# Attention with experts on one core: the pairs that scatter lose ScalarE's transfers and GpSimd's multiply, and one transfer spreads both heads' sums

## The chip, the core and the metric

The kernel runs on one core of a Trainium2 chip. The core has TensorE (PE, with PEld for the loading of weights), VectorE (DVE), ScalarE (ACT), GpSimd (POOL), SyncE (SP), which here only issues transfers, and 16 DMA engines. The metric is the device time of one launch in microseconds (us), as the median of several runs.

## The reference

A transformer block over x of shape [8, 512, 256] (8 batches, 512 tokens, 256 channels), all in float32. Cut to what matters:

```python
xn = layernorm(x)
kv = (xn @ w_kv_down) @ w_kv_up            # latent of 128, then k and v
q = xn @ w_q                               # 16 heads of 64
att = softmax(causal(q @ k.T / 8))         # per head, 512 x 512
attn = (att @ v) @ w_out
...
# experts: 8 of hidden size 128, every token takes its best 2
y = (silu(t @ gate[e].T) * (t @ up[e].T)) @ down[e].T
ffn = sum over the two experts of y * mean weight of the expert, + shared expert
return x + attn + ffn
```

## The kernel before, in words

The work on attention is cut into 64 *pairs*: 8 batches times 8 pairs of heads. The loop of line 906 goes over them, m = 0 to 63. A pair's work, with the names and lines that the profile shows:

- `keys` (L578) and `queries` (L587) multiply k and q on TensorE into PSUM, and ScalarE copies them out (L580, L592). `values` (L568) does this for v.
- `scores` (L615) multiplies q and k on TensorE, one 128-row query chunk and one head at a time. VectorE adds the causal mask and takes the row's extreme in one instruction (L622), and ScalarE takes the exponential and the row sums (L629).
- `transposed` (L642, L649) turns the 128x128 blocks in 32x32 squares on VectorE, into the tile `blk`. The squares are right inside, but lie on the wrong partitions. `moved` (L654) puts that right with 16 transfers `pt<-blk` of 80 KB, each from 32 partitions to 32 others. It gives each to a queue: SP's, GpSimd's or ScalarE's.
- `inverse_sums` (L674) takes the inverse of the row sums (L678), transposes them (`riT`, L681) and has GpSimd's queue store them as the tile `row` in DRAM (L683), 16 KB with pieces of 128 bytes.
- `spread_sums` (L686) reads `row` back, repeated over 64 partitions, into `rb`. It is two transfers on SP's queue (L691), one for each head, 128 KB each in pieces of 512 bytes.
- `weighted` (L696) multiplies the probabilities `pt` with v on TensorE (PV, `ps_y`, L704), two pairs later than their scores. ScalarE copies the result from PSUM into `yT` (L716), and GpSimd multiplies that by `rb` (L717). In the very last pair VectorE does both in one multiply from PSUM (L714).
- `project` (L729) multiplies `yT` of a whole batch with `w_out`.

The tiles `blk`, `pt` and `rb` have two buffers each, `rs` three and `row` four.

Other work is put between by a plan. `put(m, place, f)` says that f runs in pair m at a place from 0 to 2 within it. The layer norms, the router (L313) and the making of weights fill pairs 0 to 13. Then come the *scatter pairs*, m = 14 to 21. In each, four of the 32 token tiles are sent to their two experts' lists in DRAM by `scatter_rows` (L446): two indirect transfers by GpSimd (L449), each followed by a small memset (L457). From pair 22 on (E0, L885) the experts' 39 tiles are fetched, multiplied (L500, L512, L525) and added into the output in DRAM (L536), spread evenly over 67 half-pairs that begin at half-pair 49.

In a scatter pair the 16 transfers `pt<-blk` are shared so: 1 by GpSimd, 5 by ScalarE, which issues them in the next pair right after `weighted` has been called there, and 10 by SP. In other pairs it is 5 by GpSimd and 11 by SP, in the last two pairs 8 and 8. GpSimd's order of instructions is that of the program; the order within every engine follows that of the calls. In the compiled program the transfers of SP's queue take eight semaphores in turn, so that each waits for the one eight places before it to have landed; ScalarE's and GpSimd's queues do the same with theirs.

Of the kernel before, what the change touches and what calls it, by code (L numbers as in the profile page):

```python
# [32 lines left out]
F32 = mybir.dt.float32  # L33
# [7 lines left out]
P = 128  # L41
# [7 lines left out]
def kernel(  # L49
# [17 lines left out]
    nc = tc.nc  # L67

    B, T, C = x.shape
# [3 lines left out]
    D = 64  # L73
# [6 lines left out]
    NTILE = NT // P  # L80
    NQ = T // P
    VH = 4
    QB = 32
    NB = P // QB
# [9 lines left out]
    rowp = ctx.enter_context(tc.tile_pool(name="rowp", bufs=4, space=DRAM))  # L94
# [8 lines left out]
    rbp = ctx.enter_context(tc.tile_pool(name="rbp", bufs=2))  # L103
# [6 lines left out]
    def bank(shape, name):  # L110
        return ps_w.tile(shape, F32, tag="w", name=name)
# [139 lines left out]
    lats, qs, ks, vs, pts, rss, rbs, blks = {}, {}, {}, {}, {}, {}, {}, {}  # L251
    yTs, rows, shared = {}, {}, {}
# [382 lines left out]
    def transposed(b, p, i, pr):  # L635

        if (b, p) not in blks:
            blks[b, p] = blkp.tile([P, NB, 2, NBLK, QB], F32, name="blk")
        blk = blks[b, p]
        nr = min(i + 1, NQ - 1)  # L640
        for j in range(2):
            nc.vector.transpose(  # L642
                blk[:, :, j, i : i + (nr - 1) * (NQ - 1) + 1 : NQ - 1, :].rearrange(
                    "p b c q -> p c b q"
                ),
                pr[:, j, : nr * P].rearrange("p (c b k) -> p c b k", b=NB, k=QB),
            )
            if i == NQ - 1:
                nc.vector.transpose(  # L649
                    blk[:, :, j, 7, :],  # L650
                    pr[:, j, nr * P :].rearrange("p (b k) -> p b k", k=QB),
                )

    def moved(b, p, by_pool, by_act=0):  # L654


        pt = ptp.tile([P, NB, 2, NBLK, QB], F32, name="pt")

        def begin(by, k):
            a, kb = divmod(k, NB)  # L660
            by.dma_start(pt[ts(kb, QB), a], blks[b, p][ts(a, QB), kb])  # L661

        left = []
        for k in range(NB * NB):
            if k * by_pool % 16 < by_pool:
                begin(nc.gpsimd, k)
            elif k % 3 == 1 and len(left) < by_act:
                left.append(k)
            else:
                begin(nc.sync, k)  # L670
        pts[b, p] = pt
        return lambda: [begin(nc.scalar, k) for k in left]

    def inverse_sums(b, p):  # L674


        ri, riT = ris[p % len(ris)]
        nc.vector.reciprocal(  # L678
            ri[:, : 2 * NQ], rss[b, p].rearrange("p j i -> p (j i)")
        )  # L680
        nc.vector.transpose(riT, ri)  # L681
        row = rowp.tile([NB, QB, QB], F32, name="row")
        nc.gpsimd.dma_start(row.rearrange("a x q -> (a x) q"), riT)  # L683
        rows[b, p] = row

    def spread_sums(b, p):  # L686

        rb = rbp.tile([P, NB, NQ * QB], F32, name="rb")
        for j in range(2):
            row = rows[b, p][:, ts(j, NQ), :].rearrange("a i q -> a (i q)")  # L690
            nc.sync.dma_start(  # L691
                rb[ts(j, D)], row.unsqueeze(0).broadcast_to([D, NB, NQ * QB])
            )
        rbs[b, p] = rb

    def weighted(b, p, final=False):  # L696


        ps = bank([P, NB, NQ, QB], "ps_y")
        for c in range(NQ):  # L700
            for j in range(2):
                h = 2 * p + j
                at = at_ci[c, c]
                nc.tensor.matmul(  # L704
                    ps[ts(j, D), :, c:, :],
                    vs[b, h // VH][:, c, ts(h % VH, D)],
                    pts[b, p][:, :, j, at : at + NQ - c, :],
                    start=(c == 0), stop=(c == NQ - 1),
                )
        yT = ytp.tile([P, T], F32, name="yT")  # L710
        y = yT.rearrange("p (i a q) -> p a i q", a=NB, q=QB)
        rb = rbs[b, p].rearrange("p a (i q) -> p a i q", q=QB)
        if final:
            nc.vector.tensor_tensor(y, ps, rb, ALU.mult)  # L714
        else:
            nc.scalar.copy(y, ps)  # L716
            nc.gpsimd.tensor_tensor(y, y, rb, ALU.mult)  # L717
        yTs[b, p] = yT
# [48 lines left out]
    def put(m, place, f, *a):  # L767
        if place >= 2:
            m, place = m + 1, place - 2
        plan.setdefault(m, []).append((place, len(plan[m]) if m in plan else 0, f, a))  # L770

    pairs = [(b, p) for b in range(B) for p in range(NPAIR)]
    LAG = 2
    products = {}
    for m, (b, p) in enumerate(pairs):
        if m + 1 < len(pairs):
            put(m, 0.22, keys, *pairs[m + 1])
            put(m, 0.24, queries, *pairs[m + 1])
        if m < BLOCK0:
            put(m + 1, 0.32, inverse_sums, b, p)  # L780
        put(m + 1, 1.32 if m + 1 < BLOCK0 else 0.34, spread_sums, b, p)
        if m + LAG < BLOCK0:
            put(m + LAG, 1.4, weighted, b, p)
        else:
            products[m + LAG] = (b, p)
        put(m, 1.25 if m < BLOCK0 else 0.26, values, b, p * 2 // VH, p % 2)
    for b in range(B):
        m = b * NPAIR
# [82 lines left out]
    for k in range(12):  # L871
        put(R0 + k // 4, 0.35 + 0.5 * (k % 4), lambda: next(steps, None))
    S0 = R0 + 3
    for n in range(NTILE):
        put(S0 + n // NQ, 0.35 + 0.5 * (n % NQ), scatter_rows, n)


    def begin_experts():
# [3 lines left out]
        ep = tmp_pools.enter_context(tc.tile_pool(name="ep", bufs=1))  # L882
        xouts = ep.tile([P, NQ, C], F32, name="xout")

    E0 = S0 + NTILE // NQ  # L885
    END = len(pairs) - 5
    put(E0, 0.1, begin_experts)
    first, n_halves = 2 * E0 + 5, 2 * (END - E0) - 7
    for t in range(NET):
# [8 lines left out]
        put_half(2 * END + b, 0.7, bring_out, b)  # L898
    put_half(2 * END + B - 1, 0.7, bring_back)

    scattering = range(S0, S0 + NTILE // NQ)
    ordered = ExitStack()
    last = []
    rest = []
    assert BLOCK0 <= S0
    for m in range(len(pairs) + 1):
        if m == 0:
            ordered.enter_context(tc.manual_schedule(engines={nc.gpsimd.engine}))
        todo = sorted(plan.pop(m, ()), key=lambda e: e[:2])
        for g, group in enumerate(((0, 3), (1, 2)) if m < BLOCK0 else ()):  # L910
            chunks, exps = scores(*pairs[m], group)
            for chunk in last:
                transposed(*chunk)
            last = chunks
            if g == 0 and m > 0:
                moved(*pairs[m - 1], 5)
            for e in exps[:2]:
                e()
            del exps[:2]
            for place, _, f, a in todo:  # L920
                if (place >= 1) == g:
                    if place - g > EARLY:
                        while exps:
                            exps.pop(0)()
                    f(*a)
                    if exps:
                        exps.pop(0)()
            while exps:
                exps.pop(0)()
        if m < BLOCK0:  # L930
            continue

        chunks, exps = [], []
        if m < len(pairs):
            chunks, exps = scores(*pairs[m], (3, 1))
            for chunk in last:
                transposed(*chunk)
            if last:
                moved(*pairs[m - 1], 5)
            last = []  # L940
            exps.pop(0)()
            exps.pop(0)()
            transposed(*chunks.pop(0))
            weighted(*products.pop(m))
            more = scores(*pairs[m], (2, 0))
            exps.pop(0)()
            exps.pop(0)()
            transposed(*chunks.pop(0))
            chunks, exps = more
        for f in rest:  # L950
            f()
        rest = []


        for place, _, f, a in todo + [(2, 0, lambda: None, ())]:
            if place > EARLY - 0.07:
                while exps:
                    exps.pop(0)()
            if place > HALF and chunks:
                while chunks:  # L960
                    transposed(*chunks.pop(0))
                inverse_sums(*pairs[m])
                if m in scattering:
                    rest = [moved(*pairs[m], 1, 5)]
                else:
                    moved(*pairs[m], 8 if m >= len(pairs) - 2 else 5)
            f(*a)
            if exps:
                exps.pop(0)()


    weighted(*products.pop(len(pairs)))
    for tt in range(NQ):
        project(B - 1, tt, pss[tt], first=NS + NPAIR - 3, last=NS + NPAIR - 1)
    assert not plan and products.keys() == {len(pairs) + 1}, (plan, products)
    weighted(*pairs[-1], final=True)
    for tt in range(NQ):
        project(B - 1, tt, pss[tt], first=NS + NPAIR - 1)
    ordered.close()
# [45 lines left out]
```

## Time and profile before

| what | value |
|---|---|
| median of three runs | 987.74 us (986.42 to 988.87) |
| the profiled execution's own time | 987.82 us |
| its span, first to last instruction | 986.1 us |
| mean granted TensorE clock | 0.978 of full speed |
| busy: TensorE / VectorE / ScalarE / GpSimd | 933.2 / 596.4 / 506.9 / 597.5 us |
| moved by the DMA engines | 190.63 MB in 127594 packets |

The span is shorter than the time of the execution by the 1.7 us around the first and the last instruction. Busy time counts instructions that compute or that issue indirect and GpSimd transfers; issues by SP and ScalarE are in the chain of waits and the lists of transfers instead. In a row "A L1 <- B L2" the first is who waited, the second what ended the wait. "Queue" names such as q0 (GpSimd's), q1 (SP's) and q10 (ScalarE's) come with the share of the 16 DMA engines' span that their packets took. "SPq", "ACTq" and "POOLq" in the chain are the issuing of transfers by those engines.

### The profile page before, as it was taken

The page shows a single profiled execution, that of the slowest core. Times are in us where ns is not written, and L with a number is a line of the kernel's source. Part 1 is how long each engine was busy: PE and PEld are TensorE (multiplying, and loading weights), DVE is VectorE, ACT ScalarE, POOL GpSimd, SP SyncE. Part 2 cuts the span into 40 slices and gives each one's busy share as a digit, 9 for nine tenths or more (in the row PEclk, how much of TensorE's full clock was granted, in tenths as well). Part 3 has the DMA queues.
Part 4 walks back from the last instruction along what each step waited for, and adds up shares of the span by engine and source line. Part 5 has one row for each costly group of instructions (what it writes and reads, how often), then busy time and mean ns, then how long its engine had stood idle before and what let it go on. Part 6 is the DMA issues. An engine that isn't in the chain of part 4 may idle for free.

```text
span 986.1 us, 16151 instructions
## 1 busy us (share of the span) xinstructions
PE 933.2 (95%) x4326; PEld 562.6 (57%) x4326; DVE 596.4 (60%) x2160; ACT 506.9 (51%) x1468; POOL 597.5 (61%) x819
## 2 busy tenths in 40 slices
PE   8898999997679889999999999999999999999997
PEld 3454555643346435675666756576556775557555
DVE  3986783796543567446664456754567546674660
ACT  2564464544443456445664556644467544664550
POOL 2587676346677764646676566675757747665450
PEclk9899899999789999999999999999999999999999
DMA  7489788675566768867787677886778868767782
GB/s 263 124 267 307 239 280 279 169 213 170 167 185 165 203 169 227 206 148 160 197 195 204 164 164 190 209 207 157 166 181 209 202 152 193 184 151 155 194 238 79
DMA packets 127594, 190.63 MB, mean 193 GB/s; under 512 B 24896, under 2 KB 88640, under 8 KB 127264
## 3 DMA queue, kind: packets, MB, share of 16 engines
q1 hardware_dynamic: 88160, 104.28, 38.0%
q0 software_dynamic: 36864, 81.78, 34.6%
q10 hardware_dynamic: 2480, 3.55, 1.2%
q8 instruction: 35, 0.57, 0.3%
q14 instruction: 55, 0.45, 0.2%
HBM read 66.45 MB, written 50.18 MB: 118 GB/s over the span
## 4 chain that ended last, share of the span: by engine, by line
PE 76%; DMA 7%; DVE 5%; SPq 4%; ACT 3%; issue 2%; ACTq 1%; POOL 0%; another core or an unknown queue 0%; POOLq 0%; DVEq 0%
PE ps_s L615 14%; PE ps_o L729 13%; PE ps_y L704 13%; PE ps_q L587 9%; PE ps_e L512 7%; PE ps_k L578 5%; PE ps_v L568 4%; SPq L661 4%; PE ps_gu L470 3%; PE ps_ed L525 3%; DMA pt<-blk 3%; ACT pr L629 2%; PE ps_x L500 2%; PE ps_lg L297 1%; DMA rb<-row 1%
## 5 line engine op out<-in xcount | busy, mean ns | idle before, releaser
L622 DVE CUSTOM_DVE_ANT_0 ps_s<-ps_s,mask 128x128 f32<-128x128 f32 (+3 forms) x512 | 241.5, 516 | 207.9 <-PE ps_s L615 155.1
L629 ACT ACTIVATE pr<-ps_s,mn 128x128 f32<-128x128 f32 (+3 forms) x512 | 268.6, 534 | 152.8 <-DVE mn L622 125.7
L642 DVE STREAM_TRANSPOSE blk<-pr 128x384 f32<-128x384 f32 (+2 forms) x512 | 209.5, 449 | 24.6 <-ACT pr L629 15.5
L615 PE MATMUL ps_s<-k,q 64*128 64x512 f32 (+3 forms) x1024 | 189.3, 471 | 30.6 <-ACT q L592 20.8
L661 POOL DMA_DIRECT2D pt<-blk x294 | 156.4, 649 | 71.0 <-DVE ri L678 30.6
L536 POOL DMA_INDIRECT acc_d<-ye,to x78 | 127.5, 1635 | 93.5 <-issue 38.3
L704 PE MATMUL ps_y<-pt,v 128*64 128x512 f32 (+3 forms) x1024 | 157.6, 451 | 8.1 <-DVE th L462 4.2
L615 PEld LDWEIGHTS ps_s<-k,q 64*128 64x128 f32 x1024 | 92.0, 190 | 116.6 <-issue 52.5
L717 POOL TENSOR_TENSOR yT<-yT,rb 128x512 f32<-128x512 f32 x63 | 84.6, 1342 | 96.7 <-ACT yT L716 89.4
L704 PEld LDWEIGHTS ps_y<-pt,v 128*64 128x64 f32 x1024 | 70.2, 140 | 102.8 <-issue 82.9
L729 PE MATMUL ps_o<-wo_sb,yT 128*128 128x256 f32 x512 | 120.1, 380 | 2.3 <-POOL yT L717 1.5
L587 PE MATMUL ps_q<-xnT,wq_sb 128*128 128x512 f32 x256 | 121.0, 595 | 0.7 <-ACT xnT L291 0.7
L729 PEld LDWEIGHTS ps_o<-wo_sb,yT 128*128 128x128 f32 x512 | 96.9, 190 | 17.5 <-POOL yT L717 1.9
L629 ACT ACTIVATION_READ_ACCUMULATOR pr<-ps_s,mn 128x1 f32 x512 | 106.4, 208 | 0.0
L683 POOL DMA_DIRECT2D row<-riT x64 | 46.7, 729 | 58.4 <-DVE riT L681 47.7
L587 PEld LDWEIGHTS ps_q<-xnT,wq_sb 128*128 128x128 f32 x256 | 49.3, 193 | 55.5 <-issue 51.6
L512 PE MATMUL ps_e<-xgT,w 128*128 128x256 f32 x312 | 74.3, 381 | 0.1
L622 DVE DVE_READ_ACCUMULATOR2_ANT mn<- 128x1 f32 x512 | 72.6, 142 | 0.0
L449 POOL DMA_INDIRECT xg_d<-xn,at_i x64 | 62.9, 982 | 13.1 <-issue 13.1
L578 PE MATMUL ps_k<-lat,wkv_sb 128*128 128x512 f32 x128 | 69.8, 628 | 0.7 <-ACT lat L560 0.7
L512 PEld LDWEIGHTS ps_e<-xgT,w 128*128 128x128 f32 x312 | 58.7, 190 | 17.2 <-issue 5.8
L716 ACT COPY yT<-ps_y 128x512 f32<-128x512 f32 x63 | 37.1, 588 | 59.6 <-PE ps_y L704 44.1
(137 smaller groups left out, 1020.0 us busy)
## 6 DMA issues: line engine op xcount, KB each, us to landing
pt<-blk SPq DMA_DIRECT2D x690, 80.0 KB
pt<-blk POOLq DMA_DIRECT2D x294, 80.0 KB
rb<-row SPq DMA_DIRECT2D x128, 128.0 KB
xg_d<-zero POOLq DMA_DIRECT2D x26, 408.0 KB
xg<-xg_d SPq DMA_DIRECT2D x39, 272.0 KB
acc_d<-in_x_dram POOLq DMA_DIRECT2D x8, 512.0 KB
xin<-in_x_dram SPq DMA_DIRECT2D x7, 512.0 KB
xnT_d<-lnT SPq DMA_DIRECT2D x7, 512.0 KB
```

The source lines that it names most:

```text
L512: nc.tensor.matmul(ps[:, v, :], w[:, ds(at + cc * I, I)], turned[t][0][:, cc, :], start=(cc == 0), stop=(cc == NCC - 1),)
L536: nc.gpsimd.indirect_dma_start(out=acc_d[:, :], out_offset=bass.IndirectOffsetOnAxis(ap=turned[t][1][:, u : u + 1], axis=0), in_=results[t ...
L578: nc.tensor.matmul(ps, wkv_sb[:, ts(p, P)], lats[b], start=True, stop=True)
L587: nc.tensor.matmul(ps, wq_sb[:, cc, ts(p, P)], xnTs[b][:, cc, :], start=(cc == 0), stop=(cc == NCC - 1),)
L615: nc.tensor.matmul(pss[j][:, ds(at, n)], q[ts(j, D), ts(i, P)], k[ts(j, D), :n], start=True, stop=True,)
L622: nc.vector.tensor_tensor_reduce(out=pss[j][:, ds(at, n)], in0=pss[j][:, ds(at, n)], in1=mask[:, T - n :], scale=1.0, scalar=NO_MIN, op0=A ...
L629: nc.scalar.activation(o, s, AF.Exp, bias=mn, scale=-1.0, accum_out=rs[:, j, i : i + 1])
L642: nc.vector.transpose(blk[:, :, j, i : i + (nr - 1) * (NQ - 1) + 1 : NQ - 1, :].rearrange("p b c q -> p c b q"), pr[:, j, : nr * P].rearra ...
L661: by.dma_start(pt[ts(kb, QB), a], blks[b, p][ts(a, QB), kb])
L704: nc.tensor.matmul(ps[ts(j, D), :, c:, :], vs[b, h // VH][:, c, ts(h % VH, D)], pts[b, p][:, :, j, at : at + NQ - c, :], start=(c == 0), s ...
L717: nc.gpsimd.tensor_tensor(y, y, rb, ALU.mult)
L729: nc.tensor.matmul(ps, l[:, ts(tt, P)], r, start=(k == 0), stop=(k == len(ops) - 1))
```

## The change

Three things change.

1. In scatter pairs ScalarE issues no transfers: of `pt<-blk` GpSimd takes 2 and SP 14. The result of PV is multiplied by `rb` on VectorE straight from PSUM into `yT`, which takes the place of ScalarE's copy and GpSimd's multiply.
2. The scatters are spread over nine pairs, m = 14 to 22, with 3, 3, 3, 3, 5, 5, 4, 3 and 3 tiles, at even places from 0.35 on. The experts begin one pair later (E0 = 23), on 65 half-pairs from half-pair 51.
3. In all 64 pairs `row` is laid out so that each head's 512 sums are contiguous in DRAM, and one transfer on SP's queue of 256 KB, in pieces of 2 KB, spreads both heads' sums over 128 partitions. Its source is described as 2 heads by 64 repeats by 512 values. The store into `row` has its pieces in the order 4 by 32 by 32 values, with strides. `weighted` reads `rb` in the matching order.

```diff
-    def moved(b, p, by_pool, by_act=0):
-
+    def moved(b, p, by_pool):
 
         pt = ptp.tile([P, NB, 2, NBLK, QB], F32, name="pt")
...
+        for k in range(NB * NB):
             a, kb = divmod(k, NB)
+            by = nc.gpsimd if k * by_pool % 16 < by_pool else nc.sync
             by.dma_start(pt[ts(kb, QB), a], blks[b, p][ts(a, QB), kb])
...
-        row = rowp.tile([NB, QB, QB], F32, name="row")
-        nc.gpsimd.dma_start(row.rearrange("a x q -> (a x) q"), riT)
+        row = rowp.tile([QB, NB, QB], F32, name="row")
+        nc.gpsimd.dma_start(row.rearrange("x a q -> a x q"), riT)
...
-        rb = rbp.tile([P, NB, NQ * QB], F32, name="rb")
-        for j in range(2):
-            row = rows[b, p][:, ts(j, NQ), :].rearrange("a i q -> a (i q)")
-            nc.sync.dma_start(
-                rb[ts(j, D)], row.unsqueeze(0).broadcast_to([D, NB, NQ * QB])
-            )
+        rb = rbp.tile([P, T], F32, name="rb")
+        row = rows[b, p][: 2 * NQ].rearrange("(j i) a q -> j (i a q)", j=2)
+        nc.sync.dma_start(rb, row.unsqueeze(1).broadcast_to([2, D, T]))
...
-        rb = rbs[b, p].rearrange("p a (i q) -> p a i q", q=QB)
-        if final:
+        rb = rbs[b, p].rearrange("p (i a q) -> p a i q", a=NB, q=QB)
+        if by_vector:
             nc.vector.tensor_tensor(y, ps, rb, ALU.mult)
...
-    for n in range(NTILE):
-        put(S0 + n // NQ, 0.35 + 0.5 * (n % NQ), scatter_rows, n)
+
+    SHARE = (3, 3, 3, 3, 5, 5, 4, 3, 3)
+    assert sum(SHARE) == NTILE
+    for k, share in enumerate(SHARE):
+        for n in range(share):
+            put(S0 + k, 0.35 + 1.6 / share * n, scatter_rows, sum(SHARE[:k]) + n)
...
-    E0 = S0 + NTILE // NQ
+    E0 = S0 + len(SHARE)
...
-            weighted(*products.pop(m))
+            weighted(*products.pop(m), by_vector=m in scattering)
...
-                if m in scattering:
-                    rest = [moved(*pairs[m], 1, 5)]
-                else:
-                    moved(*pairs[m], 8 if m >= len(pairs) - 2 else 5)
+                moved(*pairs[m], 2 if m in scattering else 8 if m >= len(pairs) - 2 else 5)
```

More of the change, by code (lines that the diff above doesn't have):

```diff
@@ L652, in transposed @@
                 )
-    def moved(b, p, by_pool, by_act=0):
+    def moved(b, p, by_pool):
         pt = ptp.tile([P, NB, 2, NBLK, QB], F32, name="pt")
-        def begin(by, k):
+        for k in range(NB * NB):
             a, kb = divmod(k, NB)
+            by = nc.gpsimd if k * by_pool % 16 < by_pool else nc.sync
             by.dma_start(pt[ts(kb, QB), a], blks[b, p][ts(a, QB), kb])
[L663 to L668, printed above, removed]
-            else:
-                begin(nc.sync, k)
         pts[b, p] = pt
-        return lambda: [begin(nc.scalar, k) for k in left]
     def inverse_sums(b, p):
@@ L681, in inverse_sums, with weighted @@
         nc.vector.transpose(riT, ri)
-        row = rowp.tile([NB, QB, QB], F32, name="row")
-        nc.gpsimd.dma_start(row.rearrange("a x q -> (a x) q"), riT)
+        row = rowp.tile([QB, NB, QB], F32, name="row")
+        nc.gpsimd.dma_start(row.rearrange("x a q -> a x q"), riT)
         rows[b, p] = row
     def spread_sums(b, p):
-        rb = rbp.tile([P, NB, NQ * QB], F32, name="rb")
-        for j in range(2):
-            row = rows[b, p][:, ts(j, NQ), :].rearrange("a i q -> a (i q)")
-            nc.sync.dma_start(
-                rb[ts(j, D)], row.unsqueeze(0).broadcast_to([D, NB, NQ * QB])
-            )
+        rb = rbp.tile([P, T], F32, name="rb")
+        row = rows[b, p][: 2 * NQ].rearrange("(j i) a q -> j (i a q)", j=2)
+        nc.sync.dma_start(rb, row.unsqueeze(1).broadcast_to([2, D, T]))
         rbs[b, p] = rb
-    def weighted(b, p, final=False):
+    def weighted(b, p, by_vector=False):
         ps = bank([P, NB, NQ, QB], "ps_y")
@@ L899 @@
     put_half(2 * END + B - 1, 0.7, bring_back)
-    scattering = range(S0, S0 + NTILE // NQ)
+    scattering = range(S0, E0)
     ordered = ExitStack()
     last = []
-    rest = []
     assert BLOCK0 <= S0
@@ L949 @@
             chunks, exps = more
-        for f in rest:
-            f()
-        rest = []
         for place, _, f, a in todo + [(2, 0, lambda: None, ())]:
@@ L962 @@
                 inverse_sums(*pairs[m])
-                if m in scattering:
-                    rest = [moved(*pairs[m], 1, 5)]
-                else:
-                    moved(*pairs[m], 8 if m >= len(pairs) - 2 else 5)
+                moved(*pairs[m], 2 if m in scattering else 8 if m >= len(pairs) - 2 else 5)
             f(*a)
@@ L975 @@
     assert not plan and products.keys() == {len(pairs) + 1}, (plan, products)
-    weighted(*pairs[-1], final=True)
+    weighted(*pairs[-1], by_vector=True)
     for tt in range(NQ):
```

## The prediction

> **What bounds the kernel now.** I read the page first, then busy time by stage (the pairs' scores end stages: 20–228 us is pairs 0–13 with the norms and router, 228–369 the scatter pairs, 369–905 the experts, 905–945 the last light pairs). The columns after a window are its length, then each engine's busy time with its instructions, the granted clock, the DMA share and GB/s.
>
> ```profile
> PE 933.2 (95%) x4326; PEld 562.6 (57%) x4326; DVE 596.4 (60%) x2160; ACT 506.9 (51%) x1468; POOL 597.5 (61%) x819
> q1 hardware_dynamic: 88160, 104.28, 38.0%
> q0 software_dynamic: 36864, 81.78, 34.6%
> 20.00:228.00 208.00, 194.40 (x896) 108.44 (x893) 160.66 (x635) 106.62 (x313) 122.91 (x164) 0.95 0.74 225
> 228.00:369.00 141.00, 115.81 (x484) 61.41 (x483) 74.41 (x266) 60.61 (x189) 101.42 (x170) 0.92 0.65 182
> 369.00:905.00 536.00, 534.96 (x2576) 340.78 (x2575) 316.18 (x1100) 305.36 (x867) 340.17 (x415) 1.00 0.78 184
> 905.00:945.00 40.00, 38.74 (x184) 22.47 (x182) 26.87 (x101) 23.16 (x73) 16.53 (x25) 1.00 0.73 179
> ```
>
> TensorE sets the time where it is busy throughout: experts 535 of 536 us. Only the scatter stage leaves much, 25 of 141. Next to TensorE stand the 16 DMA engines, three quarters busy everywhere. That matters, because the change edits the scatter stage but also every pair's broadcast.
>
> In the scatter stage the chain of waits (start, length, what) alternates between ScalarE's queue, transfers and TensorE, and the waits of 229–369 us (total, times, longest) say who is late:
>
> ```profile
> 260.55 0.60 ACTq L661
> 261.20 0.61 ACTq L661
> 261.85 0.60 ACTq L661
> 262.97 1.94 ACT pr L629 x8
> ...
> 271.80 0.51 ACTq L661
> 273.11 4.62 DMA pt<-blk
> 278.20 1.94 ACT pr L629 x8
> ```
>
> ```profile
> ACT k L580 <- DMA pt<-blk: 12.6, 4, 4.7
> DVE ps_s L622 <- PE ps_v L568: 17.0, 4, 6.0
> PE ps_s L615 <- ACT q L592: 19.1, 6, 6.7
> ```
>
> ScalarE's five transfers queue ahead of its copy of k; a DMA semaphore holds it up to 4.7 us, and the scores behind that copy wait. DVE's lateness on masks (17 us after ps_v) is not all ScalarE's: at 276.24 us the third mask starts 4 us after its scores ended (272.03), and the lateness ends only 1 to 2.5 us after GpSimd's last scatter. So part of it follows the run of indirect transfers.
>
> **The change part by part.** A light scatter pair (15, 16, 17) takes 15.2 us; its TensorE work at full clock is about 8.3 (scores 2.5, PV 2.3, k 0.86, q 1.72, v 0.86).
>
> *ScalarE's transfers go.* 40 × 0.57 us = 23 us of issue (2.9 a pair), and the semaphore waits among them (12.6 us shown). The same 40 go to SP and GpSimd: GpSimd 1→2 a pair (+0.54 us), SP 10→14 (+4 × 0.63 = 2.5 us). SP loses one of two broadcasts (−0.63): 10 × 0.63 + 1.26 = 7.6 becomes 14 × 0.63 + 0.63 = 9.5 us a pair. Queued behind SP's four more are that pair's last pt pieces and the next broadcast.
>
> *y^T by VectorE.* Nine pairs lose ScalarE's copy (0.59) and GpSimd's multiply (1.27) and gain one VectorE multiply from PSUM (0.69, the final pair's row L714). DVE goes from 8.7 to 9.4 us in a light pair, under the others. Behind the multiply on DVE stand the next masks: if rb is not there, they wait. Before, such a wait stood on GpSimd.
>
> *Scatters.* 8 a pair (four tiles, 1.27 us each with its memset and gap = 10.2) become 6 in light pairs (7.6) and 10 in pairs 18, 19 (12.7, under 17.8 us of TensorE). GpSimd in a light pair: row 0.6 + two pt 1.1 + 7.6 + rest 0.5 = 9.8 us. Pair 22 becomes a scatter pair: 10.0 → about 10.5. The experts get 65 half-pairs instead of 67; their TensorE work is the same: 0.
>
> *If all this works*, light pairs fall to 10–10.5 us (14 to 15 us for three), pairs 20 and 21 to TensorE's 13.0 (−4), pair 14 −1 to −3, pairs 18, 19 and 22 nothing: about −20. If the lateness belongs to the scatters (1.9 us each), three light pairs keep 11.4 + 1.5: −8; if it moves with them, 0 to +6.
>
> *One broadcast instead of two.* Row first. One is seen to land 4.37 us after issue at 380.15 us. In 247–309 us, q1 took 29.2% of 62 × 16 = 992 us, 290 us. Each pt transfer costs 3.4 engine-us (q10, pt alone: 6.2% = 61.5 us for 18), 40 of them 137; the 153 left carry eight broadcasts and 0.17 MB of others: 22 to 38 engine-us a pair. I take 32, that is 2.0 us on each of 16 engines. By the row alone, 128 pieces of 2 KB in place of 512 of 512 bytes at 20 to 25 GB/s an engine (pt: 20.5) would take 11 to 13 engine-us, 0.8 us a pair: a relief in every pair.
>
> Now the rule that speaks against it. The Trainium skill, "DMA: Bandwidth & Descriptors", section "Rules for kernel authors": the number of DMA engines used is set by the slowest dimension of both patterns, so an outermost dimension of fewer than 16, such as a leading broadcast of c copies, confines the whole transfer to c engines; and a hardware queue uses the lowest-numbered ones ("Why a DMA increments its semaphore by 16 and not by 1"). Every transfer of before starts with 16, 32, 64 or 128. The new source is [2, 64 copies, 512]: two engines, the same two, 128 KB each. At 20 to 22 GB/s (20.5 in pt's row, 22 in the page's first slice, 263 GB/s at 0.74) that is 6.0 to 6.4 us of engine time. No run here shows a transfer so confined. The sum by the row is −1.2 us a pair of every engine; by the rule +4.0 of two engines. I take the rule, since nothing in the patterns contradicts it.
>
> What follows: those two engines also carry their sixteenth of all else, and each pt transfer needs all 16. Stage 1: 14.9 us a pair × 0.74 = 11.0, − 2.0 + 6.0 = 15.0, which is 101%. Experts: 36 pairs in 537 us, 14.9 × 0.78 = 11.6, + 4.0 = 15.6, or 105%: bound +25, or 0 if DMA busy time hides idle; I take +16. Stage 1: 0 to +15, I take +8. Moreover the program gives SP's transfers eight semaphores in turn, so each issue waits until the one eight before it landed (SP waited 5.3 us for rb already). With rb landing after 8 to 10 us, SP's cycle is that plus some eight issues of 0.63: 13.5 to 14.7 us for 11 pts, 15.5 to 16.5 for 14. Pairs 60–62 (9.0 us each) stretch by 4.7 each, less what the lag of two pairs cushions: +8 to +14, I take +10. The scatter stage keeps none of its 20: light pairs 15.2 → 16 (+2.4), pairs 20 and 21 as much (+1.8), pair 22 10 → 14 (+4) would make +8; where SP catches up under pairs 18 and 19, part of the earlier masks stays a gain, down to −5. I take +2.
>
> *Row store.* Same 128 pieces of 128 bytes; its first dimension is 4, so by the same rule four engines: 32 × 84 ns (q10's mean packet) = 2.7 instead of 0.7 us. SP waits for this row already 17 times in the run, 31.2 us in all (its own list of waits): +0 to +34 of SP waits, mostly inside its slack. I take 0 beside the broadcast, and keep it in the range.
>
> Sum: +8 + 2 + 16 + 10 = +36 on the profiled 987.82 us (span 986.1 and 1.7 around it; the median is 987.74): 1024.
>
> **Rivals.**
> 1. *Two engines bound* (0.58): 1024, between 1003 and 1060.
> 2. *The broadcast is spread anyway* (0.18), because the 128 destination partitions decide, or the two engines have room. For it: busy share may include waiting; against: the rule names exactly a leading dimension of c. Place: the scatter stage, price −20, no pair elsewhere lengthens: 966. It decides as soon as rb lands within some 6 us: SP's cycle is then under 10 us and GpSimd's 9.8 sets the light pair.
> 3. *Confined, but hidden* (0.13): pairs average 14.9 us and the lag evens out; only the last light pairs and SP's cycle in 15–22 pay: +13, 1001. For it: experts with TensorE 100% busy would hide landing times that stay under a pair.
> 4. *Lateness tied to scatters, broadcast spread* (0.06): −3 to +6, 985 to 994. For it: lateness ends with GpSimd's run; against: ScalarE's queue stands in the chain.
> 5. *Queueing beyond the two engines' share* (0.05): over 1060.
>
> **The numbers.** A measurement here can tell about 0.3% (3 us) from no change. Faster 0.18 is rival 2; same 0.05 comes from 3 and 4; slower 0.77. The likeliest case alone spans 1003 to 1060; the range reaches down to 972, part of rival 2, and up to 1075.
>
> **What would show it.** A rb landing of 8 us or more in the list of DMA issues and "SPq L661 <- DMA rb<-row" grown from 5.3 us to over 50 prove the confinement; a stage of experts still at 536 us with TensorE full proves rival 3; rb landing in 3 to 5 us, and fewer q1 percent, rival 2. ScalarE's waits for "DMA pt<-blk" should vanish in 229–369 us in all cases. I am wrong if pairs 23–59 do not lengthen.

## The result, and the profile after

The changed kernel took 1101.45 us as the median of four runs (1094.8 to 1102.06), beside 988.31 for the kernel before: a ratio of 1.1138 (95% interval 1.1091 to 1.1184), 113 us slower. The forecast of "slower" and its main mechanism held. The size did not: 1024 was forecast, with 1075 as the upper end.

The profiled execution took 1101.12 us, its span is 1099.2. First the rows of the page that answer to those of before.

```profile
PE 968.3 (88%) x4326; PEld 578.2 (53%) x4326; DVE 602.0 (55%) x2169; ACT 501.3 (46%) x1459; POOL 599.1 (54%) x815
q1 hardware_dynamic: 63344, 107.14, 34.1%
q0 software_dynamic: 37024, 82.29, 32.6%
```

TensorE fell from 95% to 88% of the span: it now waits. SP's queue has 25 thousand packets fewer, as the larger pieces should bring. Its 34.1% of 1099.2 us is 375 us of mean engine time, as before (38.0% of 986.1 us), but it now carries 35 more `pt` transfers. Counted over the packets in the traces, the broadcasts alone took 17.1 us of engine time a pair before (512 packets of 512 bytes, 33.5 ns each) and take 12.6 us now (128 packets of 2 KB, 98.8 ns each). So the larger pieces are cheaper, at 20.7 GB/s an engine.

Next the stages, cut at the same pairs as before (window, length, busy times, granted clock, DMA share, GB/s).

```profile
20.00:256.00 236.00, 204.39 (x895) 111.79 (x892) 161.87 (x637) 105.84 (x313) 125.90 (x165) 0.92 0.67 199
256.00:406.00 150.00, 119.57 (x489) 63.78 (x487) 77.75 (x272) 56.04 (x180) 92.36 (x163) 0.91 0.61 171
406.00:999.00 593.00, 549.38 (x2548) 347.50 (x2550) 314.38 (x1091) 302.72 (x859) 339.71 (x407) 0.97 0.70 164
999.00:1055.00 56.00, 44.08 (x206) 24.98 (x201) 31.52 (x117) 27.00 (x86) 24.89 (x34) 0.93 0.61 158
```

Against 208, 141, 536 and 40 us, the stages lost 28, 9, 57 and 16 us, and the tail 3. So half of the loss lies in the experts' stage, which the change touches only through the broadcast and by starting the experts one pair later. The mean DMA share fell everywhere, although some DMA transfer is what is waited for: a mean over 16 engines can hide a few that are full.

SP's list of waits (total, times, longest), first before, then after, and the last pairs of the chain name it.

```profile
SPq L661 <- DVE blk L642: 239.8, 50, 11.5
SPq L691 <- DMA row<-riT: 31.2, 17, 4.5
SPq L661 <- DMA rb<-row: 5.3, 7, 2.0
```

```profile
SPq L660 <- DMA rb<-row: 199.5, 46, 7.0
SPq L679 <- DMA row<-riT: 104.6, 25, 9.3
SPq L660 <- DVE blk L642: 92.8, 24, 12.1
```

```profile
1023.80 12.58 DMA rb<-row
1040.19 12.32 DMA rb<-row
1056.32 12.15 DMA rb<-row
1070.37 13.26 DMA rb<-row
```

Before, SP waited 239.8 us for VectorE's `blk`, that is, it was early; it waited 5.3 us for the broadcast. Now it waits 199.5 us for the landing of the broadcast. In the four rows of the chain some 12 to 13 us pass from issue to landing. These are late ones: over all pairs the median is 10.0 us, and eight in ten lie between 8.4 and 12.3 (4.6 us before, for each of the two). The chain before was 76% TensorE; here, near the end, it goes from one broadcast to the next, 14 to 16 us apart. Pairs took 14.58 us in the mean before (from the 919 us between the first and the last pair's reciprocals) and 16.38 after, and 63 × 1.80 = 113 us is the whole loss.

### The profile page after: what moved, and what is told of

It is laid out like the page before. It is cut to its first block, busy times and chain, and to the rows that moved or that the text cites. A ratio compares the mean times of both kernels' runs of the same rounds, so it can differ in the third digit from the quotient of the medians.

```text
span 1099.2 us, 16084 instructions
## 1 busy us (share of the span) xinstructions
PE 968.3 (88%) x4326; PEld 578.2 (53%) x4326; DVE 602.0 (55%) x2169; ACT 501.3 (46%) x1459; POOL 599.1 (54%) x815
## 3 DMA queue, kind: packets, MB, share of 16 engines
q1 hardware_dynamic: 63344, 107.14, 34.1%
## 5 line engine op out<-in xcount | busy, mean ns | idle before, releaser
L690 PE MATMUL ps_y<-pt,v 128*64 128x512 f32 (+3 forms) x1024 | 178.3, 496 | 70.0 <-DMA pt<-blk 45.4
L615 PE MATMUL ps_s<-k,q 64*128 64x512 f32 (+3 forms) x1024 | 197.3, 485 | 35.3 <-ACT q L592 21.8
L660 POOL DMA_DIRECT2D pt<-blk x299 | 160.8, 685 | 72.1 <-DVE ri L667 30.2
L690 PEld LDWEIGHTS ps_y<-pt,v 128*64 128x64 f32 x1024 | 80.5, 153 | 176.0 <-issue 134.0
L615 PEld LDWEIGHTS ps_s<-k,q 64*128 64x128 f32 x1024 | 96.5, 197 | 126.0 <-issue 54.8
L703 POOL TENSOR_TENSOR yT<-yT,rb 128x512 f32<-128x512 f32 x54 | 78.2, 1448 | 91.5 <-DMA rb<-row 51.3
L672 POOL DMA_DIRECT2D row<-riT x64 | 59.6, 931 | 59.4 <-DVE riT L670 45.1
L702 ACT COPY yT<-ps_y 128x512 f32<-128x512 f32 x54 | 31.7, 587 | 124.2 <-PE ps_y L690 115.1
```

Source lines behind the costliest of these rows:

```text
L615: nc.tensor.matmul(pss[j][:, ds(at, n)], q[ts(j, D), ts(i, P)], k[ts(j, D), :n], start=True, stop=True,)
L690: nc.tensor.matmul(ps[ts(j, D), :, c:, :], vs[b, h // VH][:, c, ts(h % VH, D)], pts[b, p][:, :, j, at : at + NQ - c, :], start=(c == 0), s ...
```

## The experiments

The theory (T): the leading 2 of the broadcast's source puts 128 KB on each of two DMA engines, and that makes the kernel slow. Its rivals: the row store in its new order is late (R), or the scatter pairs' own part costs the time (S), or one large transfer is worse than two whatever its engines (L). The runs came in five sets; in each, before ran beside them, and took 966.6, 967.2, 991.4, 966.6 and 989.2 us. So the sets differ by 2.5%, and across sets only ratios to before are compared. What makes them differ is not known: the record gives the number of one chip, 3, for the set at 966.6 with e1 to e4 and for those at 991.4 and 989.2.

### Taking the change apart

**e1_halves**, the change with two broadcasts:

```diff
-        nc.sync.dma_start(rb, row.unsqueeze(1).broadcast_to([2, D, T]))
+        for j in range(2):
+            nc.sync.dma_start(rb[ts(j, D)], row[j].unsqueeze(0).broadcast_to([D, T]))
```

> The changed kernel, with its one broadcast cut into two of 64 partitions, pieces of 2 KB as they were. Theory T (the leading 2 of the source puts 128 KB on each of two DMA engines; its 12 us landing holds SP's queue): the whole loss goes, 962 to 985 us, rb lands in 3 to 5 us. Rival R (the row store in the order 4 x 32 x 32 is late, and with it the broadcast): stays at 1060 to 1100. Rival S (the scatter pairs' own part costs the time): about 1000 or more, with pairs 14 to 22 longer than before.

962.26 us, ratio 0.9956 (0.9936 to 0.9976). One line, and the whole loss is gone.

**e2_one_only**: the kernel before with the new row layout, its reading and the one broadcast (the hunks of `inverse_sums` and `spread_sums`).

> The kernel before with the third part alone: new row layout and one broadcast of 256 KB. T and R: 1085 to 1110 us, nearly all of the loss of 113. S: about 988.

1062.81 us, 1.0987 (1.0936 to 1.1038): most of the loss, 96 us, without any edit to the scatter pairs.

**e3_scatter_only**: the change with `inverse_sums` and `spread_sums` as before.

> The change without its third part: scatter pairs as changed, row and two broadcasts of 512-byte pieces as before. T and R: faster than before by what ScalarE's queue cost, 962 to 980 us. S: over 1000.

962.21 us, 0.9966 (0.9949 to 0.9984). S falls.

**e4_layout_halves**: the kernel before with the new row layout and the two broadcasts of e1_halves.

> The kernel before with the new row layout, read by two broadcasts of 64 partitions in 2 KB pieces. T: no loss, 975 to 989 us, since a quarter of the packets cost less DMA time. R: 1060 to 1100, as the row store on its leading 4 is still there.

965.12 us, 0.9985 (0.9953 to 1.0016). The row store with a leading 4 is still in this kernel, so R falls too; and the larger pieces brought no gain that can be told from none.

### Two, four, eight, sixteen engines

Each of e1_halves' two broadcasts was described with a leading dimension of its own, of the same 64 repeats. Bytes, pieces, issues and their order stay the same; here for 2:

```diff
-            nc.sync.dma_start(rb[ts(j, D)], row[j].unsqueeze(0).broadcast_to([D, T]))
+            src = row[j].unsqueeze(0).unsqueeze(0)
+            nc.sync.dma_start(rb[ts(j, D)], src.broadcast_to([2, D // 2, T]))
```

> The kernel e1_halves with each of its two broadcasts described as 2 x 32 repeats instead of 64: same bytes, pieces, issues and order. T: a leading 2 puts each on two engines again, so the time is that of the changed kernel within some 15 us, 1055 to 1085. Rival L (the loss is that of one large transfer in place of two, or of both heads in one): stays at 962.

> As f_c2, with 4 x 16 repeats. T: four engines, 64 KB each a pair; if the landing is 2 us and the rest goes by bytes an engine (10 us at 128 KB), it lands after about 7 us and SP's cycle falls to some 12 us: 970 to 1000. L: 962.

> As f_c2, with 8 x 8 repeats. T: eight engines, 32 KB each, landing 4.5 us: 960 to 970. L: 962.

| leading dimension | kernel | time | ratio (95% interval) | median landing | load of an engine that broadcasts, and span |
|---|---|---|---|---|---|
| 2 | f_c2 | 1140.22 us | 1.1802 (1.1776 to 1.1829) | 8.8 us | 1157 of 1131 us |
| 4 | f_c4 | 1007.53 us | 1.0397 (1.0359 to 1.0436) | 6.1 us | 940 of 1014 us |
| 8 | f_c8 | 970.35 us | 1.0042 (1.0028 to 1.0057) | 4.5 us | 796 of 966 us |
| 64 | e1_halves | 962.26 us | 0.9956 (0.9936 to 0.9976) | 3.8 us | 725 of 957 us |

Nothing but the leading count differs (e1_halves ran in another set), and the time follows it. L falls, as two transfers with a leading 2 are worse than the one (f_after, below, took 1087.29 us in the same set). That the count acts through the number of engines is what the Trainium skill states ("DMA: Bandwidth & Descriptors", "Rules for kernel authors"), and the traces agree. The landing of a broadcast raises its semaphore in 2, 4, 8 and 16 separate steps for a leading 2, 4, 8 and 64 (in at least 123 of 128 broadcasts of each run). And where nothing but the changed kernel's broadcast moves, in one us near its end, the rows for all engines (window, length, busy times, granted clock, DMA share, GB/s) and for SP's queue (packets, MB, share) are:

```profile
1082.00:1083.00 1.00, 1.00 (x6) 0.45 (x6) 0.00 (x0) 0.00 (x0) 0.00 (x0) 1.00 0.13 49
q1 hardware_dynamic: 24, 0.05, 12.8%
```

12.8% of 16 engines is two engines, and 49 GB/s is some 24 an engine.

The last column of the table is an estimate. It takes the packet times of everything but the broadcast as spread evenly over 16 engines, and lays those of the broadcast on 2, 4, 8 or 16. For the changed kernel that is 688 + 405 = 1093 us for each of the two engines, of a span of 1099.2; before, it was 733 of 986.1 for each of 16. So the two engines are full nearly all the time. The estimate is good to some 5%: it comes out 2% above the span in f_c2, which was slower than expected, and whose packets took 110 ns each.

### How the slow landing reaches TensorE

Two ways were open: SP's issuing is held by the landing, since the transfer eight places behind waits for it (Q), or the two engines' own load delays what else lies on them (E).

**f_actq**: the one broadcast on ScalarE's queue (`nc.scalar` for `nc.sync`).

> The changed kernel with its one broadcast issued on ScalarE's queue instead of SP's, still from [2, 64 repeats, 512]. Theory Q (the loss comes through SP's issuing: the transfer eight places behind waits for the slow landing): SP is free again, 975 to 1015 us, with the waits SPq <- rb gone. Theory E (the two engines themselves are too full, or the pt pieces on them are late): 1050 to 1090 as before. ScalarE may lose up to 20 us where the row lands late in front of its own work.

1133.65 us, 1.1445 (1.1386 to 1.1504). It did not free SP: its list of waits still begins with the broadcast. In the trace the transfers of SP's and of ScalarE's queue take the same eight semaphores (100 to 105, 107 and 108), and so they do in the kernel before: ScalarE's queue has none of its own. GpSimd's queue has eight others (110 to 117).

```profile
SPq L660 <- DMA rb<-row: 281.1, 48, 11.7
```

**f_poolq**: the same on GpSimd's queue, whose semaphores are its own.

> The changed kernel with its one broadcast on GpSimd's queue, which has semaphores of its own; f_actq still shared SP's and so did not free SP. Theory Q (the slow landing holds SP's issuing): SP <- rb waits vanish, and the time falls well below the changed kernel's ratio of 1.12 to before, to 1.00 to 1.06. Theory E (the confined engines themselves are too slow for the pieces on them): 1.08 or more. GpSimd's own waits for the row may add some per cent to either.

1108.86 us, 1.1463 (1.1409 to 1.1517). SP was free now, with no row for the broadcast in its list and 391.3 us of waits for `blk`. But the time stayed. GpSimd's queue had taken SP's place, and TensorE waited 84.3 us for the pt pieces (45.4 in the changed kernel):

```profile
PE ps_y L690 <- DMA pt<-blk: 84.3, 26, 7.8
...
POOL pt L660 <- DMA rb<-row: 53.0, 15, 7.6
```

That run has a second difference: GpSimd's queue moved 33.8 thousand packets more for 64 broadcasts. By the trace these are 64 of 4 KB for each broadcast, which carry the data, and the rest of 8 bytes or less. Whether its two engines were the same ones all along the trace does not show.

**i_8_one**, and its control **i_8_halves** with two broadcasts: the 16 pt transfers of all pairs outside the scatter pairs shared 8 and 8, which takes three issues a pair from SP.

```diff
-                moved(*pairs[m - 1], 5)
+                moved(*pairs[m - 1], 8)
...
-                moved(*pairs[m], 2 if m in scattering else 8 if m >= len(pairs) - 2 else 5)
+                moved(*pairs[m], 2 if m in scattering else 8)
```

> The changed kernel with 8 of each pair's 16 pt transfers on GpSimd's queue and 8 on SP's, in all pairs outside the scatter pairs (5 and 11 before). Theory Q: SP's cycle is the landing of 12.4 us and the issues that come after the eighth; three issues fewer make it 16.3 - 1.9 = 14.4 us, about the pairs' 14.6 without any hold: ratio to before 1.03 to 1.08, less GpSimd's cost in the next kernel. Theory E (the two engines' load, which stays the same): 1.11 to 1.13.

> The control: the same 8 and 8 with two broadcasts over 64 partitions, which are spread over 16 engines. GpSimd issues 3 x 0.6 = 1.9 us more a pair; where its time is covered, ratio 0.995 to 1.00, else up to 1.02. Both theories agree here.

1126.16 us, 1.1391 (1.1326 to 1.1456), and 1025.58 us, 1.0318 (1.0242 to 1.0395). The control costs 3.2% by itself. Beside it the one broadcast costs 1.1391 / 1.0318 = 1.104, little less than the 1.12 (1.1138 / 0.9956) between the changed kernel and e1_halves. Q alone had promised 1.03 to 1.08. In its chain the pt pieces themselves are now late:

```profile
1077.37 11.45 DMA pt<-blk
...
1090.09 13.36 DMA rb<-row
```

So holding SP is not the whole path: with SP freed, or given fewer issues, pieces of `pt` are late instead. The load of the two engines speaks for E. In i_8_one it is, by the same estimate, 1087 of 1119 us, against 722 of 1029 in its control. In the changed kernel it is 228 of 236, 140 of 150, 615 of 593 and 54 of 56 us in the four stages. So in the experts' stage, half of the loss, the load alone covers the time. How much holding SP adds to it, there or in the other stages, stays open.

### What the scatter part is worth

**f_after**: the changed kernel again, in the set of f_c2 to f_c8.

> The changed kernel again, beside the others of this set. On the chip of e1 to e4, 1062.8 us was the third part alone; theory T (two engines, nothing else) expects 1060 to 1066 here, the scatter part's gain of 4 us or nothing. A second theory, T2, that 14 transfers of SP in the scatter pairs stand behind the slow broadcast and make them longer (22 against 17 us in pairs 19 and 20), expects 1070 to 1085.

1087.29 us, 1.1237 (1.1219 to 1.1256). That is 2.3% more than e2_one_only in a set as fast. So behind the slow broadcast the scatter part costs some 24 us, though by itself it gains 3 to 4.

**h_later_experts**: e2_one_only with only the experts one pair later.

```diff
-    E0 = S0 + NTILE // NQ
+    E0 = S0 + NTILE // NQ + 1
```

> The kernel before with the one broadcast (as e2_one_only, ratio 1.099) and the experts beginning one pair later, nothing else of the scatter part. If the later experts are what the scatter part costs behind the slow broadcast: ratio 1.115 to 1.13, as the whole change. If it is SP's 14 transfers or VectorE's multiply waiting for rb: 1.095 to 1.105.

1085.73 us, 1.1223 (1.1169 to 1.1278). That is 2.1% more than e2_one_only, so nearly all of the 2.3%: little is left for SP's 14 transfers or VectorE's wait. It is where the experts' half-pairs fall: pairs 22 to 58 end 595.0 us apart here and 592.6 in the changed kernel, 577.5 in e2_one_only and 530.2 before. Why the shift by a pair is worse behind a slow broadcast was not traced further.

**g_before**: the kernel before, for a trace in its set (991.4 us).

> The kernel before itself, for a trace on this chip: 963 to 970 us. If its scatter pairs end 110 us apart (pairs 13 to 22) as in e4 and not 130 as on the first chip, the lateness there depends on the chip, and the gain forecast from it (20 us) was read from a chip that shows more of it.

990.89 us, not the 963 to 970 that were expected from the same chip number. Pairs 13 to 22 end 135.4 us apart here and 130.1 in the trace of the prediction, but 111.0 in e4_layout_halves, which has the same scatter pairs (with the new row layout) in a set at 966.6. The lateness of the scatter pairs thus differs from set to set, and its 24 us are most of the sets' difference.

**g_noact**: the kernel before with ScalarE's transfers alone gone.

```diff
-                if m in scattering:
-                    rest = [moved(*pairs[m], 1, 5)]
-                else:
-                    moved(*pairs[m], 8 if m >= len(pairs) - 2 else 5)
+                moved(*pairs[m], 2 if m in scattering else 8 if m >= len(pairs) - 2 else 5)
```

> The kernel before with only this changed: in scatter pairs GpSimd takes 2 and SP 14 of the pt transfers, ScalarE none. If ScalarE's queue was the delay: 959 to 963 us (all of e3's gain of 3 to 4). If the multiply or the spreading of the scatters was it: 966 to 968.

979.22 us, 0.9881 (0.9844 to 0.9917), in the set at 991.4: 12 us faster, more than the whole scatter part gained in the set at 966.6.

**g_dve**: the kernel before with VectorE's multiply alone in the scatter pairs (`final=m in scattering`).

> The kernel before with only this changed: y^T of the scatter pairs by one VectorE multiply from PSUM. If GpSimd's time in the pair was the limit: 960 to 964 us; if ScalarE's queue was it: 966 to 968.

997.34 us, 1.0043 (1.0018 to 1.0067): slower by 4 us.

**h_halves**, e1_halves in another set, and **h_halves_copy**, the same with ScalarE's copy and GpSimd's multiply kept.

> e1_halves again: the change with two broadcasts of 64 partitions. On a chip where before takes 966 us: ratio 0.996. On one where before takes 988 or more and ScalarE's transfers cost 12 us (g_noact, 0.988): 0.980 to 0.988.

> h_halves with ScalarE's copy and GpSimd's multiply kept in the scatter pairs. VectorE's multiply alone measured +0.4%: if that holds beside the other parts, 3 to 4 us less than h_halves; if GpSimd's freed time is what lets fewer scatters pay, 2 to 8 us more.

962.87 us, 0.9961 (0.9942 to 0.998), and 961.71 us, 0.9954 (0.9935 to 0.9974). Both beat the kernel before by 0.4 to 0.5% in a set at 966.6. The multiply makes no difference between them that can be told. In a set near 990 us the two were not run.

## Why the prediction was right and wrong

- **The sign and the cause**: right. The rule on the leading dimension was set against the row of the trace, and the prediction chose the rule. e1_halves and the series of 2, 4, 8 and 64 bear it out.
- **What held behind it**: 20 to 22 GB/s and 6.0 to 6.4 us of engine time were right, as 64 packets of 98.8 ns are 6.3 us at 20.7 GB/s. A landing of 8 to 10 us was about right too: the median was 10.0.
- **The step that failed** is the sum of the two engines' load, in two terms, and a third beside it. The first is the old broadcast's share that falls away: "I take 32, that is 2.0 us on each of 16 engines". Its packets took 17.1 us of engine time a pair, 1.1 us on each. The working had priced SP's 40 `pt` transfers at q10's 3.4 us, where in that window they took 5.0 on SP's queue, and so left too much for the broadcasts (the packets give 82 us for the eight, not 153). The second is the charge: "bound +25, or 0 if DMA busy time hides idle; I take +16". Little was hidden. With the measured terms the experts' sum is 11.6 − 1.1 + 6.3 = 16.8 us a pair, where 16.5 was measured (593 / 36) and 15.6 forecast; that of the first stage is 11.0 − 1.1 + 6.3 = 16.2, where 16.9 was measured and 15.0 forecast. A third term was put at nothing, the experts' start one pair later ("their TensorE work is the same: 0"): behind the slow broadcast it cost 2.1% (h_later_experts).
- **SP's cycle**: with the median landing, 10.0 + some seven issues of 0.6 is 14.2 us, within the forecast of 13.5 to 14.7, but the pairs' mean was 16.38. So this cycle does not set the pair by itself, which agrees with f_poolq and i_8_one.
- **The stages**: +8, +2, +16 and +10 were taken, +28, +9, +57 and +16 measured. The first and the experts' stage, where the load was summed too low, hold 61 of the 77 us that were missing.
- **Rival 2** (spread anyway) and **rival 3** (hidden) are refuted by e1_halves and by the experts' 593 us. Rival 5, over 1060, was given 0.05. Its price came true, but its reason, queueing beyond the two engines' share, is not needed in the experts' stage, where the share alone covers the time; elsewhere it is not excluded.
- **The row store**: taken at nothing, and right by itself (e4_layout_halves, 0.9985). Beside the slow broadcast SP's waits for it grew from 31.2 to 104.6 us, which stays unexplained.
- **ScalarE's transfers**: right as to cause; their removal is worth 12 us in the set at 991.4. The forecast −20 for the scatter part without the confinement was too large for the set at 966.6, where the part measured −3 to −4. **Rival 4**, lateness that stays with the scatters, is not excluded for the rest in slower sets: in g_noact VectorE still waits 18.5 us for its masks after `ps_v` between 229 and 369 us.
- **VectorE's multiply** takes the 0.69 us that were forecast (median 692 ns), and gains nothing.

## What to carry to other kernels

Merging two transfers into one can cost far more than an issue saves when the merged pattern starts with a small count: look at the first dimension of both sides before the bytes and the pieces. Price such a transfer by what its few engines carry beside it: here 405 us of broadcasts came on top of an even share of 688, and that filled the span of 1099. The mean DMA share does not warn of this, since it fell, together with TensorE's.

## What the runs showed that was not expected

- On its two engines a packet of the broadcast takes no longer than when spread (98.8 ns for 2 KB, against 107 in e1_halves). The landing grows because each engine has eight times as many of them, among everything else that it carries: the very last broadcast, nearly alone, landed after 7.6 us.
- Moving three of eleven pt transfers a pair from SP to GpSimd costs 3.2%, though GpSimd was busy 61% of the span. In i_8_halves SP waits 239.9 us for `row`, against 31.5 in e1_halves. The row's store shares GpSimd's queue, which may be why; that was not tried apart.
- Pairs 13 to 22 take 111 us in one set (e4_layout_halves) and 130 to 135 in two others (the kernel before); elsewhere the pairs take the same time to a few us.
